# Attention's result stored by channel in four parts, products block by block, and the first chunk of x on two queues

## The chip, the core and the metric

The kernel runs on one core of a Trainium2 chip. The metric is the device time of one execution in microseconds; each version is given by the median of several executions. A profile is one execution recorded by the hardware profiler. Its times count from the first instruction of the core. PE is the engine of the matmuls, PEld its weight loads, DVE the vector engine, ACT the scalar engine, POOL GpSimd and SP the engine that only issues transfers. A "q" after a name means the engine's instruction sequencer.

## What is computed

Two blocks in sequence on x of 16 images, 1024 channels and 32 x 32 pixels, all in float32. The first is a bottleneck with local self-attention, the second an ordinary bottleneck with a 3 x 3 convolution:

```python
# block 1: 1024 -> 256 -> 1024 channels, 32 heads of 8 channels
h = relu(bn(conv1x1(x, w_conv1)))
q, k, v = relu(bn(conv1x1(h, wq))), relu(bn(conv1x1(h, wk))), bn(conv1x1(h, wv))
# for each pixel and head: 9 neighbours of k (plus position) against q, softmax, weighted sum of v
attn = softmax(einsum('bgdhw,bgdkhw->bgkhw', q, unfold3x3(k) + pos), axis=2)
a = relu(bn(einsum('bgdkhw,bgkhw->bgdhw', unfold3x3(v), attn)))
x = relu(bn(conv1x1(a, w_conv3)) + x)
# block 2: 1024 -> 256 -> 256 -> 1024 channels
o = relu(bn(conv1x1(x, w1)))
o = relu(bn(conv3x3(o, w2)))
out = relu(bn(conv1x1(o, w3)) + x)
```

## The kernel before

**Stages.** The work is cut into stages of one image, in an order written out by hand as a string of words. C (`first_conv`) makes h from x, 8 chunks of 128 channels with 4 matmuls each. Q and V (`project`) make k, q and v; P stands for C, Q and V of one image. F (`fused`) multiplies the attention's result `a` with w3, adds x and at once multiplies the result with the second block's first weights. W (`winograd_conv`) is the 3 x 3 convolution of four images, in Winograd form, and U (`last_sum`) the last 1 x 1 convolution. The order begins P0 P1 P2 P3 F0 P4 F1 and its last part is

```python
        "F12 F13 F14 U10:0123 F15 U10:4567 U11:01234 W12 U11:567 U12 U13 U14 U15",
```

PE goes through the stages one after the other. DVE does the attention of an image (`logits`, `weighted`) and the Winograd transforms beside it. A small planner (`Side`) places DVE's jobs between PE's parts with costs in microseconds while the program is built; nothing of it is left at run time. Each engine takes its instructions strictly in the order in which they were emitted.

**Products.** A tile of 256 channels lies in SBUF as two blocks of 128 channels (`NW` is 2), each of 1024 pixels. A PSUM tile holds 1024 pixels and is made in two halves of 512 pixels. A product of 256 channels with a weight is thus 4 matmuls: two blocks for each of two halves. `Expand.products` (line 386) does them for w3 and u3 (its `self.src` is `a` in F and `y` in U), `conv` in `project` (line 448) for q, k and v out of h. Both go through both blocks of one half before the other half. `reduce_part` (line 352), which makes h out of x and sums the second block's first convolution, goes through both halves of a block before the next block. ACT writes the two blocks of h by two ACTIVATEs (line 1037) and those of `a` by two in `finish_attended` (line 675). In the profile each of these matmuls is two records and each has its weight load.

**The path of attention.** DVE works on an image with a partition for each quarter of 8 rows and each head: 4 x 32 partitions, and in each 8 channels of 256 pixels. PE works with a partition for each channel. So data goes through DRAM between the two. `by_quarter` (line 438) makes such a DRAM tile; its layout is quarter, block, channel, pixel. At the end of `weighted` DVE scales the sum (line 651) and SP stores `acc` with one DMA (line 653), where each partition is one run of 8 KB. `fetch_attended` (line 661) loads it for the coming F with one DMA for each block (line 667); a partition's 4 KB come from four places of 1 KB. Then `finish_attended` puts scale, bias and ReLU on it. SP also loads all weights (`more_weights`, line 130) and stores k and v (`halo`, line 478), the Winograd forms (line 736) and the transformed weights (line 290), in the order of emission. POOL issues the loads of x, residuals and forms (`more_loads`, line 340) and the stores of results (line 418).

**The start.** ACT issues `par` (all scales and biases, line 91), and then the 8 chunks of image 0's x. SP issues w1's first 128 KB, then its other parts and more weights (`at_first` calls `more_weights` before `more_loads`). `norms`, the position table and the transformation of the Winograd weights follow.

Of the kernel before, what the change touches and what calls it, by code (L numbers as in the profile page):

```python
# [8 lines left out]
F32 = mybir.dt.float32  # L9
# [4 lines left out]
P = 128  # L14
# [4 lines left out]
NW = WID // P  # L19
# [3 lines left out]
HEAD_DIM = 8  # L23
# [3 lines left out]
NJ = 4  # L27
JROWS = H // NJ
JPIX = JROWS * W
# [4 lines left out]
G = P // HEAD_DIM  # L34
# [38 lines left out]
def sa_bottleneck_kernel(ctx: ExitStack, tc: tile.TileContext, x, w1t, wqkvt, w3t, u1t, u2t, u3t, params, out):  # L73
    nc = tc.nc
# [13 lines left out]


    par = const.tile([P, _NPAR], F32, tag="par", name="par")  # L90
    nc.scalar.dma_start(par, params)


    uw = dram.tile([NI, 3, P, NW, 2, WID], F32, tag="uw", name="uw")
# [219 lines left out]
    def more_loads():  # L314

        while loads and live[0] < CHUNKS + RESULTS - 1:
            kind, b, c = loads[0]

            spare = kind == "x" and b < 2 and c >= CHUNKS
            if live[0] >= CHUNKS and not (kind == "x" and b < 2):  # L320
                return
            if kind == "V":

                if forms.get((b, c[1] == 2), 0) < NK:
                    return
                src = form_room(b)[c[0], c[1]].rearrange("p k j e -> p (k j e)")
            elif kind == "r":
                if (b, c) not in stored:
                    return
                src = stored[b, c]  # L330
            else:
                src = x[b, c * P : (c + 1) * P, :]
            name = f"{kind}_{b}_{c}".translate(str.maketrans(" ,", "__", "()"))
            if spare:
                t = rpool.tile([P, HW], F32, tag="r", name=name)
            else:
                t = xpool.tile([P, NK * 2 * PART], F32, tag="x", name=name)
                t = t if kind == "V" else t[:, :HW]

            (nc.scalar if kind == "x" and b == 0 else nc.gpsimd).dma_start(t, src)  # L340
            loaded[loads.pop(0)] = t
            live[0] += 1

# [27 lines left out]
    class Expand:  # L371
# [13 lines left out]

        def products(self, o):
            key = piece(self.name, o * 2 // NC)
            for half in range(2):
                for n in range(NW):
                    nc.tensor.matmul(  # L390
                        self.ahead[o][:, halves(half)],
                        pieces[key][:, n, o % (NC // 2) * P :][:, :P],
                        self.src[:, n, halves(half)],
                        start=False,
                        stop=(n == NW - 1),
                        skip_group_check=True,
                    )
            if o % (NC // 2) == NC // 2 - 1:
                done_with(key)
# [44 lines left out]
    def project(b):  # L444

        h = hidden.pop(b)

        def conv(which, n):
            ps = psum.tile([P, HW], F32, tag="ps", name="ps")
            name, at = ("wqk", which * WID) if which < 2 else ("wv", 0)  # L450
            key, at = piece(name, 0), at + n * P
            for half in range(2):
                for m in range(NW):
                    nc.tensor.matmul(  # L454
                        ps[:, halves(half)],
                        pieces[key][:, m, at : at + P],
                        h[:, m, halves(half)],
                        start=(m == 0),
                        stop=(m == NW - 1),
                    )  # L460
            if n == NW - 1 and which:
                done_with(key)
            return ps

        def norm(dst, src, name, n, func):
            nc.scalar.activation(  # L466
                dst, src, func,
                bias=col(f"L0_conv_{name}_b", n), scale=col(f"L0_conv_{name}_s", n),
            )

        def halo(name, which, func):

            room, backs[name] = by_quarter(name, b, HALO, HEAD_DIM)
            for n in range(NW):
                norm(inside(kp, n), rows(conv(which, n)), name, n, func)

                block = kp[:, n]
                nc.sync.dma_start(
                    room[n], AP(block.tensor, block.offset, [block.ap[0], [JROWS * PW, NJ], [1, HALO]])
                )  # L480
                yield CHUNK

        backs = relaid[b] = {}
        q = hpool.tile([P, NW, HW], F32, tag="h", name=f"q_{b}")
        room, backs["q"] = by_quarter("q", b, JPIX, HEAD_DIM)

        def positions():

            ps = psum.tile([P, HW], F32, tag="ps", name="ps")
            for half in range(2):  # L490
                for n in range(NW):
                    nc.tensor.matmul(  # L492
                        ps[n * G * NPOS : (n + 1) * G * NPOS, halves(half)],
                        pos[:, n].rearrange("p g t -> p (g t)"),
                        q[:, n, halves(half)],
                        start=True,
                        stop=True,
                    )
            by_offset = zpool.tile([P, HW], F32, tag="z", name="by_offset")
            nc.scalar.activation(by_offset, ps, AF.Identity)  # L500

            room, backs["pos"] = by_quarter("pos", b, JPIX, NPOS)
            by_offset = by_offset.rearrange("p (j w) -> p j w", j=NJ)
            for n in range(NW):
                nc.gpsimd.dma_start(room[n], by_offset[n * G * NPOS : (n + 1) * G * NPOS])

        k = halo("bnk", 1, RELU)
        yield next(k)
        for n in range(NW):
            norm(q[:, n, :], conv(0, n), "bnq", n, RELU)  # L510
            nc.gpsimd.dma_start(room[n], q[:, n, :].rearrange("p (j w) -> p j w", j=NJ))
            yield CHUNK
        yield next(k)
        positions()
        side.add(b)
        written.add(("qk", b))
        relay("qk", b)
        yield 2.5
        for n, cost in enumerate(halo("bnv", 2, AF.Identity)):
            if n:  # L520
                written.add(("v", b))
                relay("v", b)
            yield cost
# [98 lines left out]
    def weighted(b):  # L622

        e, tree = weights_of.pop(b)
        vc = projected.pop(b)["bnv"]
        both = ppool.tile([P, 2, HEAD_DIM, JPIX], F32, tag="t", name="acc")
        acc, t = both[:, 0], both[:, 1]

        def term(k, dst):
            i, j = divmod(k, 3)  # L630
            nc.vector.tensor_tensor(  # L631
                by_row(dst),
                rows(e[:, k, :]).unsqueeze(1).to_broadcast([P, HEAD_DIM, JROWS, W]),
                vc[:, :, i : i + JROWS, j : j + W],
                ALU.mult,
            )

        if b == B - 1 and DEFERRED and DEFERRED[0] in kept:
            fetch_hidden(DEFERRED[0])
        term(0, acc)  # L640
        yield 2.3
        for k in range(1, KK):
            if k == FIRST:
                se = apool.tile([P, JPIX], F32, tag="mx", name="se")
                tree(ALU.add, se)
                nc.vector.reciprocal(se, se)
                yield 4.6
            term(k, t)
            nc.vector.tensor_add(acc, acc, t)  # L649
            yield 4.6  # L650
        nc.vector.tensor_mul(acc, acc, se.unsqueeze(1).to_broadcast([P, HEAD_DIM, JPIX]))
        summed[b], back = by_quarter("a", b, JPIX, HEAD_DIM)
        nc.sync.dma_start(back, acc.rearrange("p d w -> p (d w)"))
        make_room("v", b + 1)
        side.ready[b] = side.vector + 2.3 + RELAY
        fetch_attended()
        yield 2.3

    summed, next_fused = {}, [0]

    def fetch_attended():

        b = next_fused[0]
        if b in summed and b not in attended and b not in relu_done:
            a = attended[b] = hpool.tile([P, NW, HW], F32, tag="h", name=f"a_{b}")
            for n in range(NW):
                nc.sync.dma_start(a[:, n, :].rearrange("p (j w) -> p j w", j=NJ), summed[b][n])
            side.ready[b] = max(side.ready[b], side.tensor + 8.0)

    def finish_attended(b):  # L670
# [505 lines left out]
    made = []  # L1176

    def at_first():
        more_weights()
        more_loads()  # L1180
        norms()
        for m in range(NW):
            load_taps(m)
        load_scaled()
        scale_rows()
        for _ in range(3):
            more_weights()
        position_table()
        side.first(winograd_weights(), 24.0, 0.0)
        side.first(scale_weights(), 24.0, 0.0)  # L1190
        hooks["conv1", 2, 0] = clear_hidden
# [44 lines left out]
```

## Time and profile before

| | |
|---|---|
| time, median of 3 | 2417.11 us (2413.74 to 2418.22) |
| the profiled execution | 2414.23 us, span 2412.5 us |
| PE busy | 2381.2 us, 99% |
| DVE busy | 2080.5 us, 86% |
| ACT busy | 919.6 us, 38% |
| granted PE clock, mean | 0.998 |
| DMA | 691.04 MB, mean 286 GB/s |
| store of `acc`, 16 of 1024 KB | median 8.1 us from issue to landing |
| load of `a`, 32 of 512 KB | median 13.1 us |
| load of x on ACT's queue, 8 of 512 KB | median 12.4 us |

Busy time is the union of an engine's records; matmuls are pipelined and their ends are modelled, so a record of 592 ns stands for a matmul that lets the next one start 430 ns later. A line of waits names the engine and line that waited, then what released it, then the sum in microseconds, the number of waits and the longest. In the timeline a bracket gives the idle time of the engine just before, and what ended it. The chain of waits is followed back from the last instruction, each time to what released it.

### The profile page before, as it was taken

The numbers are of one execution on the slowest core, as the hardware profiler recorded it, in microseconds if no ns is written. First come the engines' busy times: TensorE is split into PE (matmuls) and PEld (weight loads), VectorE is DVE, ScalarE is ACT, GpSimd is POOL, SyncE is SP. The second block draws the span as 40 slices with busy tenths as digits, with TensorE's granted clock in tenths as the row PEclk, the third lists the DMA queues.
The fourth block names the chain that finished last, engine by engine and source line by source line (L and its number), as shares of the span: only waits on it lengthen the run. The fifth ranks groups of instructions, "written<-read, shape, count | busy, mean of one in ns | idle before, by whom it ended". The sixth has DMA issues, their size and how long they took to land.

```text
span 2412.5 us, 18460 instructions
## 1 busy us (share of the span) xinstructions
PE 2381.2 (99%) x6144; PEld 1149.3 (48%) x6144; DVE 2080.5 (86%) x1648; ACT 919.6 (38%) x889; POOL 467.9 (19%) x854
## 2 busy tenths in 40 slices
PE   8999999999999999999999999999999999989999
PEld 3444444444466444444466444444466444434844
DVE  4899999999999999998999999989989999873700
ACT  3323241333122574442122574334222553344265
POOL 2111111111111232111111232111111221112132
PEclk9999999999999999999999999999999999999999
DMA  9968696887798897687898997787798986788987
GB/s 355 366 211 311 240 299 211 261 296 262 270 324 271 324 393 295 234 262 240 239 312 298 309 396 279 248 281 267 237 320 300 318 328 229 245 274 273 332 297 252
DMA packets 296126, 691.04 MB, mean 286 GB/s; under 512 B 20064, under 2 KB 166496, under 8 KB 287584
## 3 DMA queue, kind: packets, MB, share of 16 engines
q0 software_dynamic: 119024, 471.40, 54.0%
q1 hardware_dynamic: 175568, 213.97, 27.8%
q10 hardware_dynamic: 1440, 4.51, 0.5%
q8 instruction: 49, 0.80, 0.1%
q14 instruction: 45, 0.37, 0.0%
HBM read 416.09 MB, written 273.70 MB: 286 GB/s over the span
## 4 chain that ended last, share of the span: by engine, by line
PE 86%; DVE 5%; issue 4%; DMA 3%; ACT 1%; POOL 1%; POOLq 0%; SPq 0%; ACTq 0%; DVEq 0%
PE ps L358 34%; PE ps L390 30%; PE ps L454 11%; PE ps L771 10%; DVE acc L631 2%; DVE acc L649 1%; PE ps L492 1%; DMA a<-a 1%; POOL out_dram L418 1%; DMA a<-acc 1%; POOL r L340 1%; ACT h L1037 1%; DMA uw<-u 0%; DMA s<-in_x_dram 0%; DVE y L797 0%
## 5 line engine op out<-in xcount | busy, mean ns | idle before, releaser
L390 PE MATMUL ps<-a,w 128*128 128x512 f32 x1024 | 460.8, 595 | 8.9 <-ACT a L675 8.9
L358 PE MATMUL ps<-result,u 128*128 128x512 f32 x1024 | 458.1, 592 | 1.3 <-ACT result L417 1.3
L358 PE MATMUL ps<-x,w 128*128 128x512 f32 x1024 | 444.5, 595 | 6.6 <-DMA x<-in_x_dram 6.6
L390 PE MATMUL ps<-y,u 128*128 128x512 f32 x1024 | 441.2, 592 | 1.0 <-ACT ps L381 1.0
L631 DVE TENSOR_TENSOR acc<-e,bnv 128x2048 f32<-128x2048 f32 x144 | 327.6, 2284 | 35.4 <-ACT e L613 32.4
L574 DVE TENSOR_TENSOR prod<-qc,bnk 128x2048 f32<-128x2048 f32 x144 | 324.1, 2287 | 1.7
L390 PEld LDWEIGHTS ps<-a,w 128*128 128x128 f32 x1024 | 195.3, 191 | 256.4 <-issue 243.4
L417 ACT ACTIVATE result<-ps,par 128x1024 f32<-128x1024 f32 x128 | 142.5, 1113 | 458.3 <-PE ps L390 397.2
L358 PEld LDWEIGHTS ps<-x,w 128*128 128x128 f32 x1024 | 195.4, 191 | 252.4 <-issue 252.4
L358 PEld LDWEIGHTS ps<-result,u 128*128 128x128 f32 x1024 | 194.3, 190 | 247.0 <-issue 237.2
L390 PEld LDWEIGHTS ps<-y,u 128*128 128x128 f32 x1024 | 194.5, 190 | 245.9 <-issue 241.3
L649 DVE TENSOR_TENSOR acc<-acc 128x2048 f32<-128x2048 f32 x128 | 293.4, 2292 | 4.4
L454 PE MATMUL ps<-h,wqk 128*128 128x512 f32 x512 | 225.8, 595 | 5.7 <-ACT h L1037 5.7
L417 ACT ACTIVATE result<-ps,bn_sh 128x1024 f32<-128x1024 f32 x127 | 141.2, 1112 | 141.2 <-PE ps L390 140.8
L418 POOL DMA_DIRECT2D r<-result x128 | 69.0, 539 | 634.6 <-ACT result L417 619.1
L579 DVE TENSOR_TENSOR prod<-prod 128x2048 f32<-128x2048 f32 (+1 forms) x80 | 166.2, 2078 | 2.5
L454 PEld LDWEIGHTS ps<-h,wqk 128*128 128x128 f32 x512 | 96.2, 190 | 132.7 <-issue 110.0
L1037 ACT ACTIVATE h<-ps,par 128x1024 f32<-128x1024 f32 x32 | 38.6, 1205 | 284.5 <-PE ps L358 284.5
L381 ACT ACTIVATE ps<-r 128x1024 f32<-128x1024 f32 x128 | 130.4, 1020 | 26.4 <-DMA r<-r 18.9
L466 ACT ACTIVATE kp<-ps,par 128x1024 f32<-128x1024 f32 x64 | 77.4, 1210 | 156.0 <-PE ps L454 127.4
L381 ACT ACTIVATE ps<-s 128x1024 f32<-128x1024 f32 x128 | 131.2, 1025 | 2.5
L340 POOL DMA_DIRECT2D x<-in_x_dram x120 | 64.0, 534 | 300.7 <-PE ps L358 229.2
(317 smaller groups left out, 2297.7 us busy)
## 6 DMA issues: line engine op xcount, KB each, us to landing
s<-in_x_dram POOLq DMA_DIRECT2D x128, 512.0 KB, 6.4
r<-result POOLq DMA_DIRECT2D x128, 512.0 KB, 4.0
r<-r POOLq DMA_DIRECT2D x128, 512.0 KB, 5.9
out_dram<-result POOLq DMA_DIRECT2D x127, 512.0 KB, 6.1
x<-in_x_dram POOLq DMA_DIRECT2D x120, 512.0 KB, 5.0
v<-v SPq DMA_DIRECT2D x96, 408.0 KB, 4.7
U<-uw SPq DMA_DIRECT2D x72, 512.0 KB, 4.8
bnk<-kp SPq DMA_DIRECT2D x32, 680.0 KB, 7.2
```

The lines of the kernel that those rows point to most:

```text
L340: (nc.scalar if kind == "x" and b == 0 else nc.gpsimd).dma_start(t, src)
L358: nc.tensor.matmul(ps[n][:, halves(half)], wt[:, c % (NC // 2), n * P : (n + 1) * P], src[:, halves(half)], start=(c == first), stop=(c == ...
L381: nc.scalar.activation(ps, loaded.pop((self.kind, self.b, o)), AF.Identity)
L390: nc.tensor.matmul(self.ahead[o][:, halves(half)], pieces[key][:, n, o % (NC // 2) * P :][:, :P], self.src[:, n, halves(half)], start=Fals ...
L417: nc.scalar.activation(to_, ps, RELU, bias=self.shift(o), scale=1.0)
L418: nc.gpsimd.dma_start(to, t)
L454: nc.tensor.matmul(ps[:, halves(half)], pieces[key][:, m, at : at + P], h[:, m, halves(half)], start=(m == 0), stop=(m == NW - 1),)
L574: nc.vector.tensor_tensor(by_row(t[:, two]), by_row(qc), kc[:, :, i : i + JROWS, j : j + W], ALU.mult)
L579: nc.vector.tensor_add(u[:, :, 0:4], u[:, :, 0:4], u[:, :, 4:8])
L631: nc.vector.tensor_tensor(by_row(dst), rows(e[:, k, :]).unsqueeze(1).to_broadcast([P, HEAD_DIM, JROWS, W]), vc[:, :, i : i + JROWS, j : j ...
L649: nc.vector.tensor_add(acc, acc, t)
L771: nc.tensor.matmul(acc[i][:, at, :, n, :], pieces[key][:, m, at, n * P : (n + 1) * P], v[:, at, :, m * (TILES + TR) :][:, :, :TILES], star ...
```

## The change

The result of attention lies in DRAM by block, channel, quarter and pixel, so that a channel is one run of 4 KB. SP stores it with one DMA for each quarter, each from 32 partitions in runs of 1 KB, and loads a block with runs of 4 KB. In `Expand.products` and in `conv` of `project` the two loops change places. The first chunk of image 0's x is loaded in two halves of 64 partitions, the first by ACT and the second by SP; `par` follows the first half on ACT; `more_loads` is called ahead of `more_weights`, so that SP's half stands before the weights.

```diff
-    nc.scalar.dma_start(par, params)
...
-            (nc.scalar if kind == "x" and b == 0 else nc.gpsimd).dma_start(t, src)
+            if (kind, b, c) == ("x", 0, 0):
+
+                nc.scalar.dma_start(t[: P // 2], src[: P // 2])
+                nc.sync.dma_start(t[P // 2 :], src[P // 2 :])
+                nc.scalar.dma_start(par, params)
+            else:
+                (nc.scalar if kind == "x" and b == 0 else nc.gpsimd).dma_start(t, src)
...
         def products(self, o):
             key = piece(self.name, o * 2 // NC)
-            for half in range(2):
-                for n in range(NW):
+            for n in range(NW):
+                for half in range(2):
                     nc.tensor.matmul(
...
             key, at = piece(name, 0), at + n * P
-            for half in range(2):
-                for m in range(NW):
+            for m in range(NW):
+                for half in range(2):
                     nc.tensor.matmul(
...
-        summed[b], back = by_quarter("a", b, JPIX, HEAD_DIM)
-        nc.sync.dma_start(back, acc.rearrange("p d w -> p (d w)"))
+
+        room = summed[b] = dram.tile([NW, P, NJ, JPIX], F32, tag=f"a{b}", name="a")
+        for j in range(NJ):
+            heads = NW * G
+            nc.sync.dma_start(
+                room.rearrange("n (g d) j w -> j (n g) d w", d=HEAD_DIM)[j], acc[j * heads : (j + 1) * heads]
+            )
...
-                nc.sync.dma_start(a[:, n, :].rearrange("p (j w) -> p j w", j=NJ), summed[b][n])
+                nc.sync.dma_start(a[:, n, :], summed[b][n].rearrange("p j w -> p (j w)"))
...
     def at_first():
+        more_loads()
         more_weights()
-        more_loads()
```

## Prediction

> **What bounds the kernel now.** I read the page first, then PE's waits, then the chain of waits in order of time around each of them, then the timeline.
>
> ```profile
> span 2412.5 us, 18460 instructions
> PE 2381.2 (99%) x6144; PEld 1149.3 (48%) x6144; DVE 2080.5 (86%) x1648; ACT 919.6 (38%) x889; POOL 467.9 (19%) x854
> PE 86%; DVE 5%; issue 4%; DMA 3%; ACT 1%; POOL 1%; POOLq 0%; SPq 0%; ACTq 0%; DVEq 0%
> ```
>
> TensorE is the bound: 31.3 us of the span are not busy, so an edit that leaves its pace alone can win only there, or where its clock was low. PE's own waits name the places:
>
> ```profile
> PE ps L390 <- ACT a L675: 8.9, 2, 5.0
> PE ps L358 <- DMA x<-in_x_dram: 6.6, 1, 6.6
> PE ps L454 <- ACT h L1037: 5.7, 13, 0.4
> PE ps L454 <- ACT by_offset L500: 1.6, 1, 1.6
> ```
>
> These are what the change aims at: line 390 (products of `a`), the first chunk of x, line 454 (products of `h`). The timeline of PE shows how line 454 loses time, here for image 0:
>
> ```profile
> 36.49 1.02 PE L454 MATMUL ps<-h,wqk 128*128 128x512 f32 x2
> 37.95 13.14 PE L454 MATMUL ps<-h,wqk 128*128 128x512 f32 x30 [0.44 <-ACT h L1037]
> ```
>
> Each matmul in the source is two records. At full pace a record takes 0.43 us (3.43 us for 8, chain of waits), so two take 0.86, but 1.46 us pass before the third starts: 0.60 us lost. ACT finishes the two blocks of `h` at 36.18 and 37.89; the second product of the old order needs the second block. The trace has 13 such places.
>
> Line 390 is lost at one place, the start of F15:
>
> ```profile
> 2113.49 4.84 DMA a<-acc
> 2118.35 0.37 SPq L667
> 2118.77 15.99 DMA a<-a
> 2134.78 1.25 ACT a L675
> 2136.07 8.85 PE ps L390 x14
> ```
>
> Before it the chain is DVE without a break from 2067.37 (acc L631, L649), released by ACT e L613, and that by PE ps L358 at 2064.30. PE ran out of work at 2126.09, did two records at 2129.95 and waited until 2136.07. The 14 records after that took 8.85 us where 14 x 0.43 = 6.0 are normal, and the granted clock is 0.68 over 2126 to 2142. The loss is 2136.07 - 2126.09 - 0.86 + 2.84 = 12.0 us, more than the waits of 8.9 us tell.
>
> **What the skill says.** The Trainium skill, "TensorE: Matmul & The Clock Gate", Part 1: an idle stretch of about 3.4 us halves the clock until PE has been busy as long again, in windows that run freely. The trace agrees: records 0.85 us apart after the wait at F15, and for the first 5 us of the kernel. "DMA: Bandwidth & Descriptors", "Queues, rings and completion order": each DMA engine takes turns between queues, a packet at a time. The trace agrees: between 2128 and 2134 POOL's queue (4 KB pieces) moved 1.96 MB and SP's (mostly the 1 KB pieces of `a`) 0.45 MB, though SP's load had been waiting since 2118.8. "SBUF — State Buffer", "Door 1: The DMA port swizzle": partitions 0 to 31 reach 8 of the 16 ports, measured there 189 GB/s for 1 MiB against 328 over 128 partitions. No DMA of the old trace shows this alone.
>
> **The change, part by part.**
>
> *Products block by block* (lines 390 and 454). The same matmuls, weight loads and waits in another order; the built program has the wait for the second block before the third matmul of a group instead of the second. Line 358 already runs in this order and takes the same 3.43 us for 8 records, so the pace stays. At each of the 13 places PE now has 4 records, 1.72 us, before it needs the second block, which came 1.46 us after the start: no wait. Gain 13 x 0.60 = **7.8 us**. ACT's own work (1.20 us a block) does not move. Bounds: 0.5 a place (6.5) to 7.8. At F15 the order gives another 0.86, counted below.
>
> *First chunk by two queues.* Before, ACT issued par at 0.80 and x at 1.24, and x landed at 6.43; SP issued w1's first part at 0.81, landed at 3.17. Now both halves of x come first, on ACT and SP, and w1's three parts and par stand behind them, each one issue (0.42 us) later. PE needs 512 + 128 KB. Data flowed from about 2.3 us; at the 366 to 419 GB/s of 4 to 8 us these take 1.7 us, with w1's rest and x's second chunk between them some 2.3, and landing takes more: PE starts near 5.1 instead of 6.57, 1.5 us earlier. Later chunks keep up: they landed 1.1 us or more ahead of PE and now have 256 KB less ahead of them on ACT's queue; w1's second half, with 256 KB more ahead of it on SP, landed at 16.43 for its use at 22.3. par is read by DVE at 3.37 for ten small operations that wait for ACT until 18.84, so its 1 us later costs nothing. But PE waits again at 53.77 (1.68 us) for a q that stands in ACT behind a wait for uw<-u, landed at 51.88; its chain goes back to PE's h, but its 11.5 us is a busy DMA queue. I count **1.0**; bounds -0.5 and 2.5, the upper with a clock window gained.
>
> *The result of attention.* SP's one store of 128 pieces of 8 KB becomes four, of 256 pieces of 1 KB and 32 partitions each; the two loads become 128 pieces of 4 KB instead of 512 of 1 KB. Three more issues for each of 16 images, at 0.42 us (a<-a was issued 0.42 apart), 1.3 us of SP each time. Behind them stand the loads of `a`, w and u, and the stores of kp. DVE's next `form` waits for the store (9.3 us, twice), PE does not wait for that DVE work: after F15 DVE idles 20.0 us for ACT vh.
>
> F15: the store landed after 4.84 us with POOL's queue idle until 2118. Now the last piece is issued 1.3 us later, and 1 MiB at the skill's 189 ("Door 1") instead of 328 GB/s is an estimated 2.3 us longer; these overlap, so +2.5: landed at 2120.8. Better bound +1, worse +8 (one slow 1 MB in 1 KB pieces is the old pair of loads, 16.4 us from issue to landing). For the loads the nearest rows are the 512 KB transfers of 4 KB pieces issued by POOL in this stretch, 6.1 to 7.8 us. First half 2127.4, second 2.3 us later (0.5 MB at half of 400 GB/s): 2129.8. ACT 1.27 each: PE resumes at 2128.7 with four records to 2130.4, waits until 2131.1. Loss 2.6 + 0.7 = 3.3 and probably no half clock, instead of 12.0: gain **8** (8.7, less something for the clock); bounds -3 and 10.5.
>
> F0: the store at 190.85 landed after 10.05 us beside POOL's loads, the halves of `a` at 208.05 and 210.08. ACT stood 4.0 and 0.7 us for them, by_offset was late, and PE waited 1.56 us at 213.40. A store later by 2.5 and loads faster by 1.5 to 2.5 cancel: **0**; bounds +1.5 and -3 (kp's next stores are behind it on SP, and ACT kp L466 waits for them). In the other 14 stages PE takes the first product 3.57 us or more after ACT has finished `a`, and 31 us or more where ACT itself had waited for the load (at 931, 1474 and 1637), so both changes are hidden there by PE's other stages.
>
> Sum: 7.8 + 1.0 + 8.0 + 0 = 16.8 us; of the span of 2412.5, 2395.7. The profiled execution itself took 2414.23, among the lower of the four shown (2413.74 to 2418.22, their middle 2415.7). Against that middle: **2399**.
>
> **The rivals.**
> 1. *The transfer is only traded*: the store loses what the load wins, F15 stays. Left: 8.8 us, 2407. For it: in a full queue 1 KB pieces get little. Against: the store at F15 meets an almost idle POOL queue, the old load a full one.
> 2. *Given back at F15*: if DVE's chain did not move with PE, PE would arrive there 8.8 us earlier and wait 8.8 more: 2408, and together with rival 1 2416, no change. Against: the chain shows DVE released by ACT, and that by PE, with 8.7 us of waiting (DVE acc L631 at 2067.37), and again at 1784.75 and 1130.19.
> 3. *Slower*: the 1 KB store under load becomes as slow as the slowest old loads (28.2 us at 837). At F0 it would land at 219 instead of 201, with ACT's queue behind it. With the store later by t at both, F0 loses t - 2 and F15 t - 7.5 (the pair of loads then lands some 9 us after the store, at 2127.3 + t instead of 2134.8): 2t - 9.5, 26.5 us for t = 18. It outweighs the 8.8 and the 4.8 us of noise from t = 11.5. With the 8.8 won elsewhere, 2433. Against: the 1 KB packets' share was still 0.92 of 2.19 MB in 2122 to 2128.
> 4. *It doesn't do what it says* (PE waits for both blocks all the same): excluded by the waits of the built program, but for ACT itself being late.
>
> **How the numbers follow.** The sum's own case 0.60 (2399), rival 1 0.27 (2407), rival 2 with rival 1 0.08 (2416), rival 3 0.05 (2433). Range: all bounds at their best give 7.8 + 2.5 + 10.5 + 1.5 = 22 off 2414, 2391; at the top the reordering alone with a loss of 3 at F0, 2411. This leaves out rivals 2 and 3. A measurement of this kernel tells 0.2%, 4.8 us, from no change. Faster 0.87 (the first two cases), same 0.08, slower 0.05.
>
> **What would show it.** Right: PE's wait for ACT h gone in 13 places; PE's first matmul near 5.1; a<-acc x64 at 256 KB and a later last landing, a<-a median well under 13.1 us; PE's waits for ACT a under 4 us and no low clock near 2130; line 390 still 592 to 595 ns a record. Wrong: a wait of 0.4 that stays, the second half of `a` at F15 landing 20 us or more after DVE's acc L651, a new PE wait for ACT kp or result in F0, or a lead of the first matmuls that is gone again at line 492.

## The result and the profile after

| | before | changed |
|---|---|---|
| time, median of 4 each | 2415.43 us (2412.76 to 2418.22) | 2440.89 us (2437.93 to 2442.21) |
| ratio, 95% interval | | 1.0104 (1.0086 to 1.0121) |
| the profiled execution | 2414.23 us, span 2412.5 | 2437.93 us, span 2436.2 |

The changed kernel is 25.5 us **slower**. The forecast was 2399 us, with 0.87 on faster. In the changed kernel the edited lines have other numbers: line 358 is now 363, 390 is 395, 454 is 459, 466 is 471, 478 is 483, 653 is 661, 675 is 685, 771 is 781 and 794 is 804; 710 is the `form` that was 700.

The page of the changed kernel: span, engines, chain.

```profile
span 2436.2 us, 18518 instructions
PE 2388.6 (98%) x6144; PEld 1154.1 (47%) x6144; DVE 2080.3 (85%) x1648; ACT 919.6 (38%) x889; POOL 466.0 (19%) x854
PE 78%; DVE 9%; DMA 7%; issue 3%; ACT 1%; POOL 1%; SPq 0%; POOLq 0%; ACTq 0%; DVEq 0%
```

PE is not busy for 47.6 us (31.3 before) and DMA's share of the chain has gone from 3% to 7%. DVE and ACT do the same work as before. So the loss is waiting, and after it some microseconds in which PE ran at half its clock (its busy time grew by 7.4 us). PE's waits say where:

```profile
PE ps L781 <- ACT z L804: 11.1, 1, 11.1
PE ps L363 <- DMA w<-in_w1t_dram: 10.1, 2, 6.6
PE ps L395 <- ACT ps L386: 8.2, 3, 5.7
PE ps L395 <- ACT a L685: 5.1, 1, 5.1
...
PE ps L459 <- ACT by_offset L505: 1.9, 1, 1.9
...
PE ps L459 <- ACT h L1047: 0.4, 1, 0.4
```

The last line is the success: the wait for h, 5.7 us in 13 places before, is down to 0.4 in one. The wait for `a` is down from 8.9 to 5.1. Three lines are new: a wait for z in W8, a second wait for w1 at the start, and a long wait for ps. PE's timeline places them:

```profile
6.62 6.16 PE L363 MATMUL ps<-x,w 128*128 128x512 f32 x8 [6.62 <-DMA w<-in_w1t_dram]
16.23 12.05 PE L363 MATMUL ps<-x,w 128*128 128x512 f32 x21 [3.45 <-DMA w<-in_w1t_dram]
...
848.61 13.59 PE L395 MATMUL ps<-y,u 128*128 128x512 f32 x24 [5.68 <-ACT ps L386]
...
1810.38 5.43 PE L781 MATMUL ps<-V__2_6527,U 128*128 128x256 f32 x16 [11.14 <-ACT z L804]
...
2156.45 9.89 PE L395 MATMUL ps<-a,w 128*128 128x512 f32 x16 [5.07 <-ACT a L685]
```

Compared matmul by matmul with the trace of before, PE is 7.3 us late after the first 65 records, 3.3 us late just before 839 us (the h places have paid back), 11.9 us late after the wait at 848, 25.3 after the one at 1810, 21.4 after F15 and 23.8 at the end. Two places, at 848 and 1810, are worth 22 us (8.6 and 13.1). What PE waits for there, ACT's ps and z, is nothing that the change touches. The chain of waits of the changed kernel shows what stands behind them:

```profile
828.41 17.94 DMA bnk<-kp
...
1711.17 12.97 DMA a<-acc
...
1780.58 10.38 DMA v<-v
...
1794.19 15.01 DMA pos<-by_offset
...
2140.89 7.28 DMA a<-acc
...
2148.32 6.81 DMA a<-a
```

At 821 us SP issues the four stores of image 5. The last lands 17.6 us after the first issue (one store before: 4.9). The store of kp, issued behind them at 828.41, needs 17.94 us (the same one before: 8.86). At 1708 us the four stores of image 12 take 16.0 us (4.1 before). What waits for them, on ACT and on DVE, first in the changed kernel, then the same first two instructions before:

```profile
846.43 1.21 ACT L471 ACTIVATE kp<-ps,par 128x1024 f32<-128x1024 f32 x1 [11.64 <-DMA bnk<-kp]
...
1724.26 1.50 DVE L710 SCALAR_TENSOR_TENSOR form<-vh 128x612 f32<-128x612 f32 x2 [11.74 <-DMA a<-acc]
...
1809.30 1.02 ACT L804 ACTIVATE z<-ps 128x1024 f32<-128x1024 f32 x1 [15.94 <-DMA pos<-by_offset]
```

```profile
834.03 1.21 ACT L466 ACTIVATE kp<-ps,par 128x1024 f32<-128x1024 f32 x1 [2.56 <-DMA bnk<-kp]
...
1700.51 1.50 DVE L700 SCALAR_TENSOR_TENSOR form<-vh 128x612 f32<-128x612 f32 x2
```

The first chain: ACT's next kp needs the buffer that the kp store frees; ACT stands 11.64 us (2.56 before), its later ACTIVATE that fills ps for line 395 is late, and PE waits. The second: DVE's `form` needs the buffer of `acc`, stands 11.74 us (the line of before has no bracket: no wait), so the transforms and their stores are late; POOL, which issues in order, stands before the load of the form V__2 until 1791, so the stores of q and pos behind it are late; pos frees the buffer that ACT's z needs, and PE waits 11.14 us for z.

### The profile page after: what moved, and what is told of

It is laid out like the page before. It is cut to its first block, busy times and chain, and to the rows that moved or that the text cites. A ratio compares the mean times of both kernels' runs of the same rounds, so it can differ in the third digit from the quotient of the medians.

```text
span 2436.2 us, 18518 instructions
## 1 busy us (share of the span) xinstructions
PE 2388.6 (98%) x6144; PEld 1154.1 (47%) x6144; DVE 2080.3 (85%) x1648; ACT 919.6 (38%) x889; POOL 466.0 (19%) x854
## 4 chain that ended last, share of the span: by engine, by line
PE 78%; DVE 9%; DMA 7%; issue 3%; ACT 1%; POOL 1%; SPq 0%; POOLq 0%; ACTq 0%; DVEq 0%
PE ps L363 30%; PE ps L395 28%; PE ps L459 10%; PE ps L781 9%; DVE acc L636 3%; DVE acc L654 2%; DMA bnk<-kp 1%; DMA a<-acc 1%; DMA w<-in_w1t_dram 1%; DVE v L710 1%; DMA U<-uw 1%; DVE form L710 1%; PE ps L497 1%; DMA v<-v 1%; DMA uw<-u 1%
## 5 line engine op out<-in xcount | busy, mean ns | idle before, releaser
L804 ACT ACTIVATE z<-ps 128x1024 f32<-128x1024 f32 x48 | 49.2, 1025 | 190.9 <-PE ps L781 133.1
```

## The experiments

The times are medians, each beside runs of the kernel before on the same chip. Ratios are to those runs. A difference of under about 0.1% tells nothing here.

**One part at a time.** Each of the three parts of the diff was put into the kernel before alone.

`e1_products`, the order of the two loops, at both places:

```diff
-            for half in range(2):
-                for n in range(NW):
+            for n in range(NW):
+                for half in range(2):
```

> The kernel before with only the order of the two loops changed in products and conv. Theory (the order saves 0.60 us at each of 13 places at line 454, about 0.9 us at F15, and nothing takes it back): 7 to 9 us faster than before, near 2407, PE's waits at line 454 for ACT h gone. Rival (PE that arrives earlier finds DVE and the transfers no earlier, so the gain is waited away later): within 2 us of before, with the waits for ACT a at F15 longer by 7 to 9 us than 8.9.

`e2_start`, the start:

```diff
-    nc.scalar.dma_start(par, params)
...
+                nc.scalar.dma_start(t[: P // 2], src[: P // 2])
+                nc.sync.dma_start(t[P // 2 :], src[P // 2 :])
+                nc.scalar.dma_start(par, params)
...
+        more_loads()
         more_weights()
-        more_loads()
```

> The kernel before with only the first chunk of x on two queues, par behind it and more_loads ahead of more_weights. Theory (SP's w1 in 1 KB pieces stands behind half of x and then gets little beside ACT's 4 KB pieces of later chunks, so its rest lands near 16 us instead of 6.75, PE waits about 3.4 us at the second chunk and runs about 7 us at half clock): 5 to 8 us slower than before, near 2422, and nearly all of it is there by 60 us. Rival (the later w1 is made up for where PE waits anyway, at 53.8 us and at F0): within 2 us of before.

`e3_path`, the store in four parts and the loads in runs of 4 KB, as in the change:

> The kernel before with only attention's result stored in four parts by channel and loaded in runs of 4 KB. Theory (the store of 1 KB runs from 32 partitions at a time lands late under load, DVE's form and SP's queue with the kp stores stand behind it, and so PE waits for ACT ps and ACT z): 20 to 26 us slower than before, near 2439, with stores of acc of 13 to 18 us from the first issue to the last landing, DMA bnk<-kp up to 18 us and waits of PE for ACT ps or ACT z of over 5 us. Rival (the waits came from PE being at another phase through the other two parts): within 5 us of before, a gain of 3 to 8 at F15 kept.

| kernel | time | before on that chip | ratio (95%) | difference |
|---|---|---|---|---|
| e1_products | 2407.81 | 2415.18 | 0.9971 (0.9961 to 0.9981) | -7.4 us |
| e2_start | 2424.09 | 2415.18 | 1.0040 (1.0028 to 1.0052) | +8.9 us |
| e3_path | 2439.14 | 2415.18 | 1.0099 (1.0086 to 1.0112) | +24.0 us |

The sum is +25.5 us, what the whole change costs. The parts hardly touch each other. The theories of e1 and e3 met their times; e2 came out slightly over its upper end of 8 us, and in its profile 9.0 of the 9.1 us are lost by 60 us, as its theory said. The rival of e3, that the waits came from PE being in another phase, is out: e3 alone has PE's wait for z (11.8 us) and for ps (6.3 us).

**Which stores.** If two stores do the damage, the other 14 are free. In `e6_all_but_two` images 5 and 12 keep the old store and load, and the others have the new; `e6b_only_two` is the reverse:

```diff
+        if b in (5, 12):
+            summed[b], back = by_quarter("a", b, JPIX, HEAD_DIM)
+            nc.sync.dma_start(back, acc.rearrange("p d w -> p (d w)"))
+        else:
+            room = summed[b] = dram.tile([NW, P, NJ, JPIX], F32, tag=f"a{b}", name="a")
...
```

> The kernel before with attention's new store and loads for 14 images, images 5 and 12 as before. Theory (the delay sits at two places, where kp stores stand behind image 5's store and DVE's form waits for image 12's, worth 9 and 12 us of the path's 24.0): within 1 to 6 us slower than before, PE's waits for ACT ps at 839 us and ACT z at 1787 us gone. Rival (any slower store delays something, and the waits only move to the next place): over 12 us slower.

> The kernel before with attention's new store and loads for images 5 and 12 alone. Theory (these two stores bring the waits of PE for ACT ps at 839 us and for ACT z at 1787 us): 17 to 22 us slower than before. Rival (those two waits need the delays that the stores of the images before them added up): within 8 us of before.

e6_all_but_two: 2415.23 against 2415.64, ratio 0.9999 (0.9993 to 1.0006): **nothing**. e6b_only_two: 2439.73, 1.0105 (1.0091 to 1.0118), +24.1 us: **all of it**. PE's waits of e6b_only_two, where the lines have moved again (783 and 806 are the changed kernel's 781 and 804; 390, 381 and 687 are its 395, 386 and 685):

```profile
PE ps L783 <- ACT z L806: 12.2, 1, 12.2
PE ps L390 <- ACT a L687: 8.1, 2, 4.5
PE ps L390 <- ACT ps L381: 6.6, 2, 5.6
```

The wait for z and the wait for ps are there again; the wait for `a` is F15's old one. So 2 of 16 stores cost 24 us, and the remaining 14, F0 and F15 among them, come out at zero together. Both expectations were a little off in size (+1 to +6 and +17 to +22 were given).

**What about the store is slow.** It was changed in two ways: it is cut into four DMAs of 32 partitions, and its runs went from 8 KB to 1 KB. Four kernels separate them. All have the old loads in pieces of 1 KB, except e5.

`e4_four_long`: cut by partitions, runs of 8 KB.

```diff
-        nc.sync.dma_start(back, acc.rearrange("p d w -> p (d w)"))
+        for j in range(NJ):
+            heads = slice(j * NW * G, (j + 1) * NW * G)
+            nc.sync.dma_start(back[heads], acc[heads].rearrange("p d w -> p (d w)"))
```

> The kernel before with the store cut into the same four DMAs of 32 partitions, but in the old layout with runs of 8 KB, and the old loads of 1 KB runs. If the cut into 32 partitions and three more issues is what costs: slower by over 10 us, four-part stores of over 12 us under load, as in the changed kernel. If the 1 KB runs of the store cost: within 4 us of before, stores about as long as before plus 1.3 us.

`e11_one_padded`: not cut, but runs of 1 KB, because the rows in DRAM are padded.

```diff
+        t = dram.tile([NJ, NW, P, JPIX + 64], F32, tag=f"a{b}", name="a")[:, :, :, :JPIX]
+        summed[b] = t.rearrange("j n c w -> n c j w")
+        nc.sync.dma_start(t.rearrange("j n (g d) w -> (j n g) d w", d=HEAD_DIM), acc)
```

> The kernel before with attention's store as one DMA from all 128 partitions, but to rows with a pitch of 1280 bytes, so that its pieces are of 1 KB instead of 8 KB; the loads keep their 1 KB pieces. If 1 KB runs alone lose the start before POOL's queue fills: over 8 us slower, image 5's store over 10 us and image 12's over 8 us from issue to landing (4.9 and 4.1 before). If it takes the cut into 32 partitions: within 4 us of before, those two stores under 7 us.

`e13_four_wide`: cut into four DMAs, each over all 128 partitions.

```diff
+        for j in range(NJ):
+            part = slice(j * HEAD_DIM // NJ * JPIX, (j + 1) * HEAD_DIM // NJ * JPIX)
+            nc.sync.dma_start(back[:, part], acc.rearrange("p d w -> p (d w)")[:, part])
```

> The kernel before with attention's store cut into four DMAs by channels instead of by quarters: each takes two of the eight channels of all 128 partitions, in runs of 2 KB; layout and loads as before. If what costs in the cut by quarters (16.6 us with runs of 8 KB) is that each DMA takes only 32 partitions: within 5 us of before, image 5's store under 7.5 us and image 12's under 7 us from first issue to last landing (10.5 and 10.8 in the cut by quarters). If it is that there are four DMAs with their issues: over 10 us slower, those stores over 9 us.

`e5_one_short`: the new layout and loads, the store as one DMA from 128 partitions by a pattern of four dimensions.

```diff
+        to = AP(room.tensor, room.offset, [[JPIX, NJ], [HEAD_DIM * HW, NW * G], [HW, HEAD_DIM], [1, JPIX]])
+        nc.sync.dma_start(to, acc)
```

> The kernel before with the new layout of attention's result, its store of 1 KB runs and its loads of 4 KB runs, but the store as one DMA from all 128 partitions. If the cut into four DMAs of 32 partitions costs most (the same cut with runs of 8 KB cost 16.6 us of the path's 24.0) and the runs the rest: 4 to 10 us slower than before, first issue to last landing of the store near 10 to 11 us. If the 1 KB runs are what is slow and the cut only repeats it: over 14 us slower, stores near 13 us. If the cut alone costs: within 4 us of before.

| kernel | runs, partitions of one DMA | store of image 5 / 12, us | ACT kp waits | DVE form waits | ACT z waits | time to before |
|---|---|---|---|---|---|---|
| before | 8 KB, 128 | 4.9 / 4.1 | 2.6 | 0 | 0 | |
| e13_four_wide | 2 KB, 128 | 10.8 / 8.1 | 7.3 | 3.9 | 4.7 | 1.0006 (0.9998 to 1.0014) |
| e11_one_padded | 1 KB, 128 | 5.4 / 7.0 | 7.0 | 2.7 | 4.3 | 1.0012 (1.0003 to 1.0021) |
| e4_four_long | 8 KB, 32 | 10.5 / 10.8 | 9.6 | 6.5 | 12.1 | 1.0067 (1.0053 to 1.0080) |
| e3_path | 1 KB, 32 | 16.5 / 15.8 | 12.3 | 11.5 | 17.3 | 1.0099 (1.0086 to 1.0112) |

(The waits are those at 826 to 848, at 1700 to 1726 and, for pos, at 1787 to 1813 us of each profile, the stores from first issue to last landing.) PE's waits in e4 for z and ps, and then the one for ps in e13, which has none for z:

```profile
PE ps L773 <- ACT z L796: 7.3, 1, 7.3
PE ps L390 <- ACT ps L381: 4.7, 2, 3.7
```

```profile
PE ps L390 <- ACT ps L381: 3.1, 4, 1.4
```

It is above all the 32 partitions that cost: four issues over 128 partitions cost nothing that can be told apart from zero, runs of 1 KB from 128 partitions cost 3.4 us, with an interval that only just leaves out none, and the cut by partitions costs 16.6 us even with runs of 8 KB. With both it is 24.0. No run separates the last 7.4 us into runs and new loads, but the profiles do: at the two places PE loses 3.9 and 10.3 us in e4 and 9.2 and 13.8 in e3, and the loads of image 5 were issued at 848.43 in e3, when ACT's wait there was over.

In time e4 and e13 met their first cases. The stores did not: e4's took 10.5 and 10.8 us, not over 12, and e13's 10.8 and 8.1, not under 7.5 and 7. At image 5 the stores of e4 and e13 are about equally long, so the length of the store alone is not the price. Two other things differ. One is the time that the DMA engines spend on it: summed over its packets, the store of image 5 took 52 us of them before, 49 in e13, 52 in e11, 66 in e3 and 78 in e4. The other is that the chains have slack. With waits of about 7 us on ACT for the kp store and about 4 on DVE for `acc` (e13, e11) PE waits at most 1.4 us at a time for ps or z; with 6.5 us on DVE it waits 7.3 for z, with 11.5 it waits 11.8.

The stretch of image 12's store shows what 32 partitions mean (columns: time, engines' busy time, PE's clock, the share of time in which the DMA engines are busy, GB/s). First two short stretches in which nothing but this store moves, before and then e4_four_long:

```profile
1697.00:1699.50 2.50, 2.50 (x7) 1.07 (x6) 2.50 (x2) 0.16 (x1) 1.06 (x2) 1.00 1.06 406
```

```profile
1700.60:1701.80 1.20, 1.20 (x4) 0.48 (x3) 1.20 (x1) 0.14 (x1) 0.71 (x2) 1.00 1.04 218
```

Then six microseconds in which POOL's transfers run beside it, e4_four_long and e13_four_wide:

```profile
1701.00:1707.00 6.00, 6.00 (x16) 2.65 (x15) 3.17 (x2) 1.53 (x2) 1.22 (x3) 1.00 0.91 200
```

```profile
1701.00:1707.00 6.00, 6.00 (x15) 2.66 (x14) 3.72 (x2) 1.31 (x2) 1.11 (x3) 1.00 0.95 318
```

(A share just over 1 means that packets overlap a little in the records.) The DMA engines are as busy in e4 as before and move about half of the bytes, and beside POOL's transfers some six tenths of what they move in e13. In the packet records a packet of 8 KB of this store takes 344 ns on average before and 634 in e4. And before, the megabyte was through in 3 us, while POOL's queue was only starting; in e4 and e3 most of it still stood there when POOL's packets of 4 KB came (10.9 KB for bnv later), and took turns with them. The Trainium skill, "SBUF — State Buffer", "Door 1: The DMA port swizzle", was drawn on in the prediction for the half of the ports that 32 partitions reach; these two runs agree with it (218 against 406 GB/s). "DMA: Bandwidth & Descriptors", "Rules for kernel authors", advises one transfer over 128 partitions instead of two over halves, since they share the DMA engines; for quarters the 16.6 us that e4 loses agree, beside 0.5 us for e13's four transfers over all 128.

e5_one_short was meant as the clean counterpart and is not: 2565.02 us, 1.0634 (1.0614 to 1.0655), far beyond even the second case's 14 us and stores of 13 us. Its SP queue at image 5:

```profile
859.97 0.54 SPq L655 DMA_DIRECT2D a<-acc  x1
860.61 21.68 SPq L130 DMA_DIRECT2D w<-ws  x1
```

The next issue on SP took 21.68 us, and in the 22 us the DMA engines were busy for 0.67 of the time. Pieces of 1 KB from 128 partitions are cheap in e11, so it is this pattern (four dimensions, 4 outermost) that is slow. The packet records show how: of this store never more than 6 packets were under way at once, 2.5 on average while any was; of e11's store of image 5 up to 20, and 13.6 on average. So it was served by few of the 16 DMA engines. No run varies the outermost 4, so that it sets their number is not shown.

**The start.** `e15_half` has only the halves of x, par stays first; `e14_par` has only par behind x.

> The kernel before with only the first chunk of x in two halves, the second on SP ahead of the weights; par first on ACT as before. If the half of x on SP's queue is the whole cost: 7 to 11 us slower than before, w1's rest landed near 16 us and PE's wait at the second chunk over 3 us. If par's place has a share: 2 to 6 us slower.

> The kernel before with only par behind the first chunk of x on ACT's queue, the chunk whole as before. If par's place costs (the operations on bn_inv, row and the weights that wait for it start later, and ACT and uw behind them): 3 to 7 us slower than before, PE's wait for q at 54 us longer than 1.7. If only the half of x on SP's queue costs: within 2 us of before, PE's first matmul near 6.2 us.

e15_half: 2424.23 against 2415.80, 1.0035 (1.0023 to 1.0047), +8.4 us. e14_par: 2417.04, 1.0004 (0.9994 to 1.0014), nothing clear of the noise, though its wait for q grew to 3.50 us. So half of x on SP ahead of the weights is the cost, and par is not, or by no more than the interval. PE's timeline in e15_half:

```profile
5.99 5.78 PE L363 MATMUL ps<-x,w 128*128 128x512 f32 x8 [5.99 <-DMA w<-in_w1t_dram]
14.47 10.54 PE L363 MATMUL ps<-x,w 128*128 128x512 f32 x24 [2.69 <-DMA w<-in_w1t_dram]
```

PE starts 0.6 us sooner and then waits for w1's rest, 2.69 us where over 3 had been expected. SP's queue (q1) in the window 2 to 8 us, before and then changed (columns: packets, MB, share):

```profile
q1 hardware_dynamic: 830, 0.82, 42.8%
```

```profile
q1 hardware_dynamic: 428, 0.60, 39.0%
```

and all three queues of the changed kernel from 8 to 16 us, where q0 is POOL's and q10 ACT's:

```profile
q0 software_dynamic: 328, 1.64, 52.2%
q10 hardware_dynamic: 332, 1.23, 38.8%
q1 hardware_dynamic: 336, 0.33, 11.8%
```

Before, SP's 0.82 MB hold all of w1's first 512 KB. Changed, 0.26 of the 0.60 MB are x, so some 0.18 of w1's 0.52 MB are left when POOL's queue begins to move at 8 us. From then on each queue gets about the same number of packets, and SP's are of 1 KB: 0.33 MB in 8 us, 41 GB/s. The last of w1's first half lands at 16.10 (6.75 before), when 0.33 MB have moved: by then some DMA engines were already at the next transfer.

Two attempts to keep the early start without this:

`e12_w1_first`: half of x on SP, but behind w1's first 512 KB.

```diff
                 nc.sync.dma_start(view[:, part], src[:, part])
+            while second:
+                nc.sync.dma_start(*second.pop())
```

> The kernel before with the changed start, but with SP's half of x behind the first 512 KB of w1 instead of ahead of it. Theory (w1's 1 KB pieces must be through before POOL's queue starts near 8 us): w1's rest landed by 8 us, PE's first matmul between 6.5 and 8.5 us, no wait at the second chunk, within 3 us of before. Rival (a half of x on SP delays w1 in either order): w1's rest after 10 us and 5 to 9 us slower, as with the changed start alone.

`e8_half_pool`: the second half of x on POOL, with the products block by block.

```diff
+                nc.scalar.dma_start(t[: P // 2], src[: P // 2])
+                nc.gpsimd.dma_start(t[P // 2 :], src[P // 2 :])
+                nc.scalar.dma_start(par, params)
```

> The kernel before with the products block by block, and the first chunk of x in two halves on ACT and POOL, par behind the first half, w1 first on SP as before. Theory (what cost at the start is w1 behind half of x on SP, so that its rest met POOL's queue): PE's first matmul between 5.0 and 6.2 us, w1's rest landed by 8 us, no wait of PE at the second chunk, and in all 7 to 9 us faster than before. Rival (half of x on a second queue starves w1 wherever it is issued): w1's rest after 10 us and the time 3 us or more above the 2407.8 of the products alone.

In both w1's rest landed early, at 5.95 and 6.01, and PE did not wait at the second chunk, as the theories said. Neither held its time. e12_w1_first took 2422.25 against 2413.44, 1.0031 (1.0019 to 1.0043), +8.8 us: x's second half landed at 8.12, so PE started at 8.25 (6.57 before), and at 58 us it waited 4.30 us for q instead of 1.7:

```profile
8.25 30.10 PE L365 MATMUL ps<-x,w 128*128 128x512 f32 x64 [8.25 <-DMA x<-in_x_dram]
...
58.09 3.29 PE L499 MATMUL ps<-q,pos 128*64 128x512 f32 x6 [4.30 <-ACT q L473]
```

These two are 4.3 us; with half clock after the wait PE is 5.7 us late at 60 us, and its profiled execution, the fastest of seven, ends 5.7 us later than before's. ACT's q stood 5.96 us behind a DMA uw<-u there. What the other executions lose is open. In time e12 thus lies with its rival: w1's late rest is what costs in e2 and e15, where the trace shows PE waiting for it, but bringing w1 in time does not win the loss back. e8_half_pool took 2413.62 against 2415.64, ratio 1.0000 (0.9992 to 1.0008): the 7.4 us of the products are lost. POOL first worked on a memset, issued its half at 3.36, and it landed at 10.95, where PE started, 4.4 us later than before. Its profile also has a wait of 3.95 us near 335 us for ACT's result, far from the edit.

**The best version.** F15 gains in the change's profile, so `e10_last_only` has the products everywhere and the new path for image 15 alone:

```diff
+        if b < B - 1:
...
+        else:
+            room = summed[b] = dram.tile([NW, P, NJ, JPIX], F32, tag=f"a{b}", name="a")
...
```

> The kernel before with the products block by block everywhere, and attention's new store and loads for image 15 alone. Theory (the new path is worth 3 to 5 us at F15 and costs at other places only): 10 to 13 us faster than before, near 2404, the waits for ACT a at F15 under 5 us and the last half of a landed by 9 us after the store. Rival (with the order of products there is nothing more to win at F15): 7 to 8 us faster, near 2408.

2408.76 against 2413.44, 0.9980 (0.9973 to 0.9987), -4.7 us: neither case, and no better than e1_products. At F15 the loss is 9 to 10 us in both profiles, first e1_products, then e10_last_only:

```profile
2123.43 3.78 PE L390 MATMUL ps<-a,w 128*128 128x512 f32 x4 [3.65 <-ACT a L675]
2129.50 7.15 PE L390 MATMUL ps<-a,w 128*128 128x512 f32 x12 [2.29 <-ACT a L675]
```

```profile
2131.01 9.37 PE L390 MATMUL ps<-a,w 128*128 128x512 f32 x16 [6.63 <-ACT a L687]
```

With the half clock after them these are 10.0 and 9.1 us. Block by block, the old loads serve: ACT gets the first half of `a` 15.0 us after DVE's last operation on `acc` and the second after 21.0, and the first feeds four records while the second is under way. With the new path it is 18.0 and 20.5 us: the first half comes later by more than the second comes sooner. What else differs in e10's profile is a wait of 4.6 us near 330 us, long before the edit acts. Waits of 3.3 to 4.0 us for the same thing (ACT's result in an early F) stand in the profiles of e3, e4, e6, e8 and e13 too, so it probably belongs to the execution. The version to keep is e1_products, 0.9971 (0.9961 to 0.9981) of before; by the two ratios the changed kernel takes 1.3% more, about 32 us.

## Why the prediction was wrong

- **Products block by block**: right. 7.8 us forecast, 7.4 measured alone, in which some 2 us of F15 stand that the forecast counts elsewhere; all 13 waits are gone in e1_products, 12 in the changed kernel.
- **First chunk by two queues**: wrong in sign, 1.0 won forecast, 8.9 lost. The failed step is "PE needs 512 + 128 KB" together with "Later chunks keep up": it followed w1's first 128 KB and its second half, and counted the 384 KB between them only as traffic, without asking when they land, though the second chunk needs them. They landed at 16.10 instead of 6.75. It took the 366 to 419 GB/s of 4 to 8 us for granted and did not ask what SP's 1 KB pieces get once POOL's queue runs. The earlier start did not come either: w1's first 128 KB, behind x on SP, landed at 6.49 and set PE's first matmul at 6.62.
- **The result of attention, F15**: right in sign, half in size. The wait was 5.07, and the 16 records after it took 2.9 us more than at full clock, so 8.0 us were lost, against 3.3 forecast and 12.0 before. Two terms were mis-sized. The store's "+2.5" is 4.6: it took 9.4 us from first issue to last landing where one store took 4.84. And "probably no half clock" is 2.9 us. The loads were forecast well: 7.0 and 9.7 us after the store, against 6.6 and 9.0.
- **The other stages**: this is the failed step that cost most. It reads "In the other 14 stages PE takes the first product 3.57 us or more after ACT has finished `a`, [...] so both changes are hidden there", and so puts the path outside F0 and F15 at nothing. This looks only at who reads `a`. The 24 us come from two who do not: those that stand behind the store on SP (the kp store, and behind it ACT in order) and the one who needs its source buffer (DVE's `form`). The prediction named both. It dismissed the second with "PE does not wait for that DVE work: after F15 DVE idles 20.0 us", which is true at F15 and not at W8, where z, through POOL's order, hangs on the transforms; and it priced the first under F0 only.
- **Rival 3, slower**: right in that the store becomes slow under load and ACT's queue stands behind it, and near in its price (the path alone cost 24.0 where the rival reckoned with 26.5), but wrong in its place, so the nearness of the price is luck. F0 and F15 together with 12 other images cost nothing. And it put the slowness down to the 1 KB pieces, where the cut into 32 partitions costs more.

## What to carry to other kernels

When a transfer is made slower, do not only ask who reads what it brings: list what stands behind it on its queue, who needs the buffer it frees, and follow each in every stage in which it occurs, to the first engine with no slack. A slower store can cost nothing (14 of 16 together here) or some 8 to 15 us, by the slack behind it. If a store has to be cut, cut it so that each DMA still takes all partitions: four DMAs of 32 partitions cost 16.6 us here, four over 128 cost nothing measurable. Pieces of 1 KB beside two queues of larger pieces got a packet's turn here, not a share of the bytes, so ask of weights in small pieces when the last of them lands; but putting them first only moved the loss elsewhere (e12).

## What the hardware showed that was not expected

- Stores from 32 partitions keep the DMA engines as busy as one from 128 and move about half: 218 GB/s at a share of 1.04, against 406 at 1.06. Beside other traffic all queues together moved 200 GB/s, against 318 with the cut over 128 partitions.
- One DMA with a pattern of four dimensions, the outermost of 4, had at most 6 packets under way at image 5 and held the next issue on SP for 21.68 us. With 16 such stores and the new loads the kernel took 149 us longer.
- The price of a wait is more than the wait. After the 3.45 us at the start PE's clock was half from 15.0 to 21.9 us, after the 5.68 us at 848 from 847.9 to 854.7, and there PE lost 8.6 us in all. A wait of 1.94 us was enough for 3.4 us of half clock: PE resumed at 218.66, and from 219.8 to 223.3 its clock was half.
